# One transfer for four partition groups, and rings of rows without repeated rows, in an involution-like convolution layer

## The chip, the cores and the metric

The kernel runs on one core of a Trainium2 chip. The metric is the device time of one execution in microseconds (us). Before the change the median of three timed runs is 3795.8 us (3777.51 to 3800.52). One more execution was recorded by the hardware profiler; its own time is 3790.98 us, and the page and the trace spoken of below are of that one.

## The reference

The program has two layers. The first is the one the change is in. For each image it normalises `x` by groups, makes three 1x1 convolutions `x1` (32 channels), `x2` (32) and `x3` (256), and computes a weight for each of 49 neighbours of each pixel. The weights are shared by the 8 channels of a group.

```
sub2 = x1[:, :, None] - unfold_patches(x2)          # 7x7 neighbours, reflected edges
feat = concat([sub2, subp])                         # subp: the same of two position planes
y    = relu(bn1(feat));  y = conv1x1(y, cw1)
y    = relu(bn2(y));     wgt = softmax(conv1x1(y, cw2) + cb2, over the 49 neighbours)
out += x3p[:, :, i:i+56, j:j+56] * wgt[:, :, idx]   # for the 49 (i, j), x3p = x3 padded
x    = x + out
```

There are 4 images of 256 channels and 56 x 56 pixels. The second layer is attention and a routed feed-forward network over the pixels as tokens. The change does not touch it.

## The kernel before

**The 49 neighbours.** The 128 partitions are four groups of 32 channels. Group g holds the same channels for another neighbour: a slot is a place (ki, kj) and a way, and group g of it works on kj+g (way `COLUMN`) or ki+g (way `ROW`). Twelve slots (`SLOTS`) of four groups are 48 neighbours. The 49th, the centre, is worked on apart: the functions named `..._own`.

**Blocks.** An image is cut into 14 blocks of 4 rows; 56 blocks in all. One round of a block reads the planes of `x1` and `x2`, takes differences (GpSimd), makes the hidden layer and the logits (TensorE into the PSUM tile `quad`, ScalarE out of it), the softmax, and then for each slot a product of a window of `x3` with the weights (`product_t`: eight slots on VectorE, the four of `POOLS` on GpSimd) which TensorE sums over the groups into `acc` (`add_t`). `divide` takes the sum out of `acc` into the tile `o`, `more` adds `x`, and `store` writes the block to `xs`.

**Planes in HBM, rings in SBUF.** For every 8 rows of an image `planes` computes `x1`, `x2` and `x3`, and `store_both` and `store_values` write them, padded, to `a12d` and `x3d` in HBM. The blocks load them back shifted by group: `rows_kept` fills the rings `xc` and `xw` (windows of `x3` for the two ways, 8 channels per partition) and `ac` (of `x2`). A ring keeps 12 rows, and its first three rows a second time behind them, so that every window of 4 rows is contiguous. Each load is four transfers, one for each group of 32 partitions, because each group reads from another offset. Every transfer is issued by SyncE's queue. `load_own` loads the middle row group of `x3` once more (`x3c`), for the centre's product, and the block's part of `x` (`xr`).

One transfer already has another form: `a1`, `aq` and the main transfer of `store_values` each move all 128 partitions, and the side of the transfer that lies in HBM is written as four groups of 32 rows. This is the main one of `store_values`:

```
bass.AP(to.tensor, to.offset, [[2 * PITCH, 4], list(to.ap[0]), [1, 2 * PITCH]])
```

**The order.** Every step of a round has a place in the table `AT`, in units of which a round has `ROUND` = 238. Step s of block k stands at `k * ROUND + AT[s]`; all steps are sorted by it and written down in that order, and each engine and SyncE's queue keep it (`InOrder`). Because the recording helper issues every operation, nearly all of them have its line, L946, in the profile; tiles tell them apart. On SyncE's queue the transfers of several blocks and of the next image's planes lie one behind another, stores among loads, and a transfer that waits holds up those behind it.

Of the kernel before, what the change touches and what calls it, by code (L numbers as in the profile page):

```python
# [58 lines left out]
def bn_affine(nc, pool, par, n, eps, tag):  # L59
# [25 lines left out]
KEPT = 12  # L85
RING = KEPT + 3
# [14 lines left out]
ROUND = 238  # L101
AT = {
    "load_places": -32, "load_relation": -13, "load_planes": -5, "differ_0": 0, "differ_1": 8,
    "differ_2": 11, "normal_0": 14, "normal_1": 19, "bend_0": 27, "differ_3": 31, "values_0": 43,
    "keep_values_0": 70, "differ_own": 81, "bend_1": 87, "load_statistics": 93, "stats": 98,
    "both": 104, "bend_own": 118, "hidden_0": 140, "keep_both": 151, "edges_both": 175,
    "bend_more_0": 179, "hidden_1": 201, "bend_more_1": 214, "load_second": 215, "logits_0": 227,
    "hidden_own": 241, "largest_0": 244, "bend_more_own": 253, "store_both": 253,
    "logits_own": 258, "logits_1": 264, "keep_own": 264, "values_1": 267, "largest_1": 271,
    "keep_values_1": 278, "most": 287, "lower_own": 290, "edges_values": 292, "spread_most": 316,  # L110
    "keep_most": 319, "lowered_0": 334, "exp_0": 343, "lowered_1": 344, "weights_0": 352,
    "load_first": 352, "store_values": 354, "weights_1": 355, "product_0": 360, "exp_own": 362,
    "product_1": 364, "product_2": 370, "exp_1": 373, "weights_3": 384, "add_up": 391,
    "product_5": 391, "weights_4": 393, "product_3": 394, "add_0": 410, "weights_6": 433,
    "invert": 435, "add_1": 436, "spread_inverse": 444, "add_3": 445, "product_4": 448,
    "keep_inverse": 458, "load_third": 466, "product_6": 479, "add_2": 484, "weights_7": 485,
    "add_6": 491, "product_8": 494, "add_5": 497, "weights_9": 500, "product_7": 504,
    "load_own": 505, "product_11": 514, "add_4": 519, "weights_10": 527, "product_own": 528,
    "product_9": 530, "product_10": 537, "add_8": 540, "add_7": 555, "shift_own": 565,
    "add_own": 574, "add_9": 580, "add_11": 587, "add_10": 592, "divide": 603, "more": 672,  # L120
    "store": 760,
# [4 lines left out]
def conv_layer(ctx: ExitStack, tc: tile.TileContext, d, xs: bass.AP, ln0: bass.AP):  # L126
# [72 lines left out]
    held = {}  # L199
# [80 lines left out]
    def planes(n, q):  # L280
# [92 lines left out]
        def store_values():  # L373
            stag = made.pop("x")
            to = x3d[n, :, (PAD + 8 * q) * PITCH : (PAD + 8 * q) * PITCH + 1]
            sy.dma_start(
                bass.AP(to.tensor, to.offset, [[2 * PITCH, 4], list(to.ap[0]), [1, 2 * PITCH]]),
                stag.rearrange("p h s w -> p (h s w)"),
            )
            for i in range(PAD):  # L380
                for copied, row, to in ((over, PAD - i, i), (under, 6 - i, WP - PAD + i)):
                    if copied:
                        sy.dma_start(
                            x3d[n, :, to * PITCH : (to + 1) * PITCH],
                            stag[group(row // 2), row % 2].rearrange("p s w -> p (s w)"),
                        )
# [35 lines left out]
    mean_w = const.tile([P, P], F32, name="mean_w")  # L422
# [8 lines left out]
    xc = rings.tile([P, RING, SH, WP], F32, name="xc")  # L431
    xw = rings.tile([P, RING, SH, WP], F32, name="xw")
    ac = rings.tile([P, RING, WP], F32, name="ac")
# [3 lines left out]
    quarters = lambda a, n, j: a[n].rearrange("(l j s) f -> j l s f", j=4, s=2)[j]  # L437
# [7 lines left out]
    def rows_kept(n, quads, ring, of, way):  # L445

        count = ROW_QUADS if way == ROW else COL_QUADS
        height = WP - PAD if way == ROW else WP
        pitch = of.shape[-1] // WP
        every = pitch if way == ROW else 1  # L450
        ring = ring.rearrange("p h s w -> p (h s w)" if ring is not ac else "p h w -> p (h w)")
        todo, quads = [], list(quads)
        while quads:
            at = (count * n + quads[0]) * 4 % KEPT
            m = min(len(quads), (KEPT - at) // 4)
            rows = min(4 * m, height - 4 * quads[0])
            todo.append((at, 4 * quads[0], rows))
            quads = quads[m:]
        for at, r, rows in list(todo):
            if at == 0:  # L460
                todo.append((KEPT, r, min(rows, RING - KEPT)))
        for at, r, rows in todo:
            for g in range(4):
                size = rows * pitch - (g if way == COLUMN else 0)
                from_ = r * pitch + g * every
                sy.dma_start(
                    ring[group(g), at * pitch : at * pitch + size], of[:, from_ : from_ + size]
                )

    def first_row(k, t):  # L470

        ki, _, way = SLOTS[t]
        n, b = blocks[k]
        return (4 * ((ROW_QUADS if way == ROW else COL_QUADS) * n + b) + ki) % KEPT

    def load_relation(k):
        n, b = blocks[k]
        at = (b * RB + PAD) * WP
        a1 = ap.tile([P, RB, WP], F32, tag="a1", name=f"a1_{k}")
        src = a12d[n, :, 0, at : at + RB * WP]  # L480
        sy.dma_start(
            a1.rearrange("p h w -> p (h w)"),
            bass.AP(src.tensor, src.offset, [[0, 4], list(src.ap[0]), [1, RB * WP]]),
        )
        rows_kept(n, [b + 2] if b else range(3), ac, a12d[n, :, 1], COLUMN)
        aw = ap.tile([P, WINDOW, WP], F32, tag="aw", name=f"aw_{k}")
        for g in range(4):
            off = (b * RB + g) * WP
            sy.dma_start(
                aw[group(g)].rearrange("p h w -> p (h w)"),  # L490
                a12d[n, :, 1, off : off + WINDOW * WP],
            )
        aq = ap.tile([P, 2, W], F32, tag="aq", name=f"aq_{k}")
        for i in range(2):
            src = a12d[n, :, i, at + PAD : at + PAD + 1]
            sy.dma_start(
                aq[:, i],
                bass.AP(src.tensor, src.offset, [[WP, RB], list(src.ap[0]), [1, W]]),
            )
# [9 lines left out]
    def load_first(k):  # L509
        n, b = blocks[k]  # L510
        rows_kept(n, [b + 2 if b else 0], xc, x3d[n], COLUMN)

    def load_second(k):
        n, b = blocks[k]
        if b == 0:
            rows_kept(n, (1, 2), xc, x3d[n], COLUMN)
        if b == 0:
            rows_kept(n, [0], xw, x3d[n], ROW)

    def load_third(k):  # L520
        n, b = blocks[k]
        rows_kept(n, [b + 1], xw, x3d[n], ROW)

    def load_own(k):
        n, b = blocks[k]
        at = b * RB + PAD
        x3c = xrp.tile([P, RB, 2, WP], F32, tag="x3c", name=f"x3c_{k}")
        xr = xrp.tile([P, 2, FB4], F32, tag="xr", name=f"xr_{k}")
        for j in range(4):
            sy.dma_start(  # L530
                x3c[group(j)].rearrange("p h s w -> p h (s w)"),
                x3d[n].rearrange("l (h f) -> l h f", f=PITCH)[
                    :, at : at + RB, 2 * j * WP : 2 * (j + 1) * WP
                ],
            )
        for j in range(4):
            sy.dma_start(
                xr[group(j)], quarters(x, n, j)[:, :, b * FB4 : (b + 1) * FB4]
            )
        held["x", k] = x3c, xr  # L540

    def relation(k):
# [4 lines left out]
        def differ(i):  # L547
# [5 lines left out]
            else:  # L553
                r = first_row(k, t)
# [11 lines left out]
        def differ_own():  # L566
            aq = held["a", k][2]
            c = held["c1", k] = smp.tile([P, W], F32, tag="c1", name=f"c1_{k}")
            gp.tensor_tensor(c, aq[:, 0], aq[:, 1], ALU.subtract)
# [56 lines left out]
    def softmax(k):  # L626
# [42 lines left out]
        def lower_own():  # L669
            w = held["rw", k] = smp.tile([P, 2, W], F32, tag="rw", name=f"rw_{k}")  # L670
            ve.tensor_tensor(
                w[:, 1], held["mm", k][:, 2], held["mx", k], ALU.subtract
            )

        def exp_own():
            w = held["rw", k][:, 1]
# [27 lines left out]
        def add_up():  # L704
# [9 lines left out]
            for q in range(4):  # L714
                te.matmul(
                    small[group(q), :W], spreads[:, q, :REL], held["rw", k][:, 1], start=False,
# [3 lines left out]
        def invert():  # L720
            z = smp.tile([P, W], F32, tag="z", name=f"z_{k}")
            ve.tensor_reduce(z, view(small, 0, [[1, W], [W, 4]]), AX.X, ALU.add)
            ve.reciprocal(held["rw", k][:, 0], z)

        def spread_inverse():
            rw = held["rw", k]
            for q in range(4):
                for j in range(4):
                    te.matmul(
                        view(small[group(j)], q * W, [[FB4, 2], [1, W]]),  # L730
                        spreads[:, q, group(j)], rw, start=True, stop=True,
                        skip_group_check=True,
                    )

        def keep_inverse():
            r = held["rzs", k] = smp.tile([P, 2, FB4], F32, tag="rzs", name=f"rzs_{k}", bufs=1)
            se.activation(r.rearrange("p i f -> p (i f)"), small[:, : 2 * FB4], AF.Identity)
# [24 lines left out]
    def values(k):  # L762
# [7 lines left out]
        def product(t):  # L770
# [8 lines left out]
            (ve if ours else gp).tensor_tensor(  # L779
                pr.rearrange("p s (h w) -> p s h w", w=W),  # L780
                (xw if way == ROW else xc)[:, r : r + RB, :, kj : kj + W].rearrange(
                    "p h s w -> p s h w"
                ),
# [1126 lines left out]
```

## Time and profile before

| | |
|---|---|
| median of three timed runs | 3795.8 us |
| profiled execution: own time, span | 3790.98 us, 3789.2 us |
| convolution layer, from the start to the last `divide` | 1891 us |
| attention and feed-forward, after it | 1898 us |
| PE, DVE, ACT, POOL busy over the span | 84%, 63%, 42%, 46% |
| bytes moved by DMA, mean rate | 376.40 MB, 99 GB/s |

The span runs from the first to the last of the program's instructions. PE is TensorE, DVE VectorE, ACT ScalarE, POOL GpSimd, SP SyncE. The page's DMA share is the mean busy share of the core's 16 DMA engines, so four busy engines make 0.25. The busy shares are means over two layers with different limits, so they say little of the convolution alone; the windows over parts of the span do.

### The profile page before, as it was taken

The numbers are of one execution on the slowest core, as the hardware profiler recorded it, in microseconds if no ns is written. First come the engines' busy times: TensorE is split into PE (matmuls) and PEld (weight loads), VectorE is DVE, ScalarE is ACT, GpSimd is POOL, SyncE is SP. The second block draws the span as 40 slices with busy tenths as digits, with TensorE's granted clock in tenths as the row PEclk, the third lists the DMA queues.
The fourth block names the chain that finished last, engine by engine and source line by source line (L and its number), as shares of the span: only waits on it lengthen the run. The fifth ranks groups of instructions, "written<-read, shape, count | busy, mean of one in ns | idle before, by whom it ended". The sixth has DMA issues, their size and how long they took to land. (4 is left out here: it accounts for less than half of the span.)

```text
span 3789.2 us, 124795 instructions
## 1 busy us (share of the span) xinstructions
PE 3182.8 (84%) x55008; PEld 1437.2 (38%) x55008; DVE 2390.2 (63%) x3050; ACT 1585.4 (42%) x2880; POOL 1758.1 (46%) x1165
## 2 busy tenths in 40 slices
PE   2888876788678895898889988998899889979989
PEld 1333322333233342333244334333433344336666
DVE  2688666787678884788865557655665476534211
ACT  2455544454345453454324543454244424532111
POOL 0677656776577775788752015122421153111311
PEclk7899888899889897999989999999999999989999
DMA  5666656666666665666410220122012200231110
GB/s 142 154 165 148 165 127 156 165 151 155 146 161 159 160 144 135 158 163 157 111 66 20 63 53 27 29 77 61 29 22 73 68 24 12 60 94 44 53 50 27
DMA packets 251148, 376.40 MB, mean 99 GB/s; under 512 B 108041, under 2 KB 216237, under 8 KB 250221
## 3 DMA queue, kind: packets, MB, share of 16 engines
q1 hardware_dynamic: 236413, 333.79, 36.4%
q0 software_dynamic: 11408, 32.32, 2.7%
q8 instruction: 431, 7.06, 0.8%
q10 hardware_dynamic: 2784, 2.30, 0.2%
q14 instruction: 112, 0.92, 0.1%
HBM read 299.06 MB, written 68.74 MB: 97 GB/s over the span
## 5 line engine op out<-in xcount | busy, mean ns | idle before, releaser
L946 PE MATMUL acc<-pr,same 128*32 128x448 f32 x5376 | 644.5, 575 | 133.8 <-POOL pr L946 71.2
L946 ACT ACTIVATE ph<-pg,unit 128x896 f32<-128x896 f32 x448 | 427.1, 1004 | 473.8 <-PE pg L946 473.2
L946 POOL TENSOR_TENSOR pr<-xc,w 128x1792 f32<-128x1792 f32 x112 | 413.4, 3702 | 218.6 <-ACT w L946 141.3
L946 POOL TENSOR_TENSOR pr<-xw,w 128x1792 f32<-128x1792 f32 x112 | 422.5, 3773 | 148.8 <-PE acc L946 124.4
L946 DVE TENSOR_TENSOR pr<-xc,exp 128x1792 f32<-128x1792 f32 x224 | 443.3, 1999 | 51.0 <-ACT exp L946 44.9
L946 DVE TENSOR_TENSOR pr<-xw,exp 128x1792 f32<-128x1792 f32 x224 | 445.2, 2007 | 0.0
L946 POOL TENSOR_TENSOR phi<-ls 128x512 f32<-128x512 f32 (+1 forms) x200 | 245.6, 1228 | 350.0 <-PE accs L946 184.5
L946 DVE TENSOR_TENSOR phi<-pv,ls 128x1408 f32<-128x1408 f32 (+1 forms) x200 | 321.9, 1619 | 64.9 <-PE accs L946 47.7
L946 PE MATMUL quad<-y,cw 32*32 32x448 f32 (+1 forms) x10752 | 308.9, 476 | 13.3 <-ACT w L946 5.9
L946 DVE TENSOR_REDUCE mm<-quad 128x56 f32<-128x1792 f32 x112 | 174.1, 1554 | 217.3 <-PE quad L946 212.8
L946 PE MATMUL pg<-qT,pairs 32*128 32x448 f32 x1792 | 275.0, 591 | 6.2 <-ACT ph L946 3.8
L946 POOL DMA_DIRECT2D out<-tk x28 | 20.9, 747 | 541.7 <-ACT tk L946 531.1
L946 PEld LDWEIGHTS acc<-pr,same 128*32 128x32 f32 x5376 | 147.0, 114 | 322.3 <-issue 131.7
L946 POOL TENSOR_TENSOR y<-a,ac 128x672 f32<-128x672 f32 x112 | 168.1, 1524 | 204.8 <-DMA a<-a12d 102.0
L946 PE MATMUL pv<-wqkv,xn 128*32 128x256 f32 x3136 | 218.3, 394 | 49.6 <-DVE phi L946 31.2
L946 ACT ACTIVATE ls<-pv 128x256 f32<-128x256 f32 (+1 forms) x200 | 77.5, 387 | 390.7 <-PE pv L946 347.8
L946 PE MATMUL accs<-phi,v 128*32 128x512 f32 (+1 forms) x1600 | 218.9, 611 | 23.2 <-DVE phi L946 22.2
L946 ACT ACTIVATE exp<-w 128x224 f32<-128x224 f32 x448 | 158.3, 357 | 179.8 <-DVE pr L946 178.3
L946 POOL DMA_INDIRECT us<-rows,to x112 | 110.6, 987 | 263.1 <-DMA us<-rows,to 232.4
L946 ACT ACTIVATE y<-quad,bn2t,bn2s 128x1792 f32<-128x1792 f32 x112 | 164.7, 1470 | 139.1 <-PE quad L946 136.9
L946 PE MATMUL acc<-ph,cf 128*32 128x448 f32 (+1 forms) x1792 | 215.5, 553 | 0.0
L946 ACT ACTIVATE w<-quad,par 128x1792 f32<-128x1792 f32 x112 | 154.5, 1379 | 104.5 <-PE quad L946 101.5
(273 smaller groups left out, 5393.6 us busy)
## 6 DMA issues: line engine op xcount, KB each, us to landing
xw<-x3d SPq DMA_DIRECT2D x224, 248.0 KB
xw<-x3d SPq DMA_DIRECT2D x96, 186.0 KB
x3d<-sx SPq DMA_DIRECT2D x28, 496.0 KB
x3c<-x3d SPq DMA_DIRECT2D x224, 62.0 KB
xc<-x3d SPq DMA_DIRECT2D x54, 248.0 KB
xc<-x3d SPq DMA_DIRECT2D x54, 247.9 KB
xc<-x3d SPq DMA_DIRECT2D x54, 247.8 KB
xc<-x3d SPq DMA_DIRECT2D x54, 247.6 KB
```

The source lines that it names most:

```text
L946: return lambda *a, **k: self.tc.keep_in_program_order(of(*a, **k))
```

## The change

- `rows_kept` becomes `rows_shifted`: one transfer for all four groups, the HBM side written as four groups of 32 rows. The loads of `aw`, `ac`, `xc` and `xw` use it, and `store` writes a block in two transfers of 128 partitions in place of four of 32.
- `xc` keeps 20 rows and `xw` 16, without a second copy of the first three. A window that goes past the end of the ring is cut: `product` then issues two instructions, and a quad (4 rows) is loaded one block earlier.
- The centre's product reads row `PAD` of the ring `xw` in a layout of [group: row, 8 channels], so `x3c` is no longer loaded. Its sum takes 16 small matmuls in place of 4, and the inverse is spread once and not with a second weight beside it.
- `xr` is loaded from an input that the host lays out by block, in one contiguous transfer of 128 partitions. `aq` has one part in place of two.
- New places (`AT`, `ROUND` = 236); an image's planes are prepared six rounds ahead, not four; the statistics of image 1 run at twice the pace.

```diff
-KEPT = 12
-RING = KEPT + 3
+COL_KEPT, ROW_KEPT = 20, 16
+AC_KEPT = 12
+AC_RING = AC_KEPT + 3
...
-ROUND = 238
+ROUND = 236
...
-    def rows_kept(n, quads, ring, of, way):
...
-        for at, r, rows in list(todo):
-            if at == 0:
-                todo.append((KEPT, r, min(rows, RING - KEPT)))
-        for at, r, rows in todo:
-            for g in range(4):
-                size = rows * pitch - (g if way == COLUMN else 0)
-                from_ = r * pitch + g * every
-                sy.dma_start(
-                    ring[group(g), at * pitch : at * pitch + size], of[:, from_ : from_ + size]
-                )
+    def rows_shifted(n, r, rows, to, of, way):
...
+        size = rows * pitch - (PAD if way == COLUMN else 0)
+        sy.dma_start(
+            to[:, :size],
+            spread_out(
+                of, r * pitch, [[pitch if way == ROW else 1, 4], list(of.ap[0]), [1, size]]
+            ),
+        )
+
+    def load_quad(i, way):
+        count, height, kept, ring = (
+            (ROW_QUADS, WP - PAD, ROW_KEPT, xw) if way == ROW else (COL_QUADS, WP, COL_KEPT, xc)
+        )
+        n, q = divmod(i, count)
+        rows = min(4, height - 4 * q)
+        at = 4 * i % kept
+        rows_shifted(
+            n, 4 * q, rows, ring[:, at : at + rows].rearrange("p h s w -> p (h s w)"), x3d, way
+        )
...
     def load_relation(k):
...
-        for g in range(4):
-            off = (b * RB + g) * WP
-            sy.dma_start(
-                aw[group(g)].rearrange("p h w -> p (h w)"),
-                a12d[n, :, 1, off : off + WINDOW * WP],
-            )
...
+        rows_shifted(n, b * RB, WINDOW, aw.rearrange("p h w -> p (h w)"), a12d, ROW)
...
     def load_own(k):
         n, b = blocks[k]
-        at = b * RB + PAD
-        x3c = xrp.tile([P, RB, 2, WP], F32, tag="x3c", name=f"x3c_{k}")
-        xr = xrp.tile([P, 2, FB4], F32, tag="xr", name=f"xr_{k}")
-        for j in range(4):
-            sy.dma_start(
-                x3c[group(j)].rearrange("p h s w -> p h (s w)"),
...
-        held["x", k] = x3c, xr
+        xr = held["x", k] = xrp.tile([P, 2, FB4], F32, tag="xr", name=f"xr_{k}")
+        sy.dma_start(xr.rearrange("p s f -> p (s f)"), d["x_own"][n, b])
...
         def spread_inverse():
-            rw = held["rw", k]
-            for q in range(4):
-                for j in range(4):
-                    te.matmul(
-                        view(small[group(j)], q * W, [[FB4, 2], [1, W]]),
-                        spreads[:, q, group(j)], rw, start=True, stop=True,
-                        skip_group_check=True,
-                    )
+            spread(held["rz", k])
...
+            ring, kept = (xw, ROW_KEPT) if way == ROW else (xc, COL_KEPT)
+            rest = max(0, r + RB - kept)
+            for h, at, rows in ((0, r, RB - rest), (RB - rest, 0, rest)):
+                if rows:
+                    f = slice(h * W, (h + rows) * W)
+                    (ve if ours else gp).tensor_tensor(
...
         def product_own():
-            pr = made["own"] = smp.tile([P, 2, FB4], F32, tag="po", name=f"po_{k}", bufs=1)
+            pr = made["own"] = smp.tile([P, SH, W], F32, tag="po", name=f"po_{k}", bufs=1)
+            r = (4 * (ROW_QUADS * n + b) + PAD) % ROW_KEPT
             ve.tensor_tensor(
-                pr.rearrange("p s (h w) -> p s h w", w=W),
-                held["x", k][0][:, :, :, PAD : PAD + W].rearrange("p h s w -> p s h w"),
...
+                pr, xw[:, r, :, PAD : PAD + W],
+                held["wo", k].unsqueeze(1).to_broadcast([P, SH, W]), ALU.mult,
             )
...
         def store():
-            xr = held.pop(("x", k))[1]
-            f = slice(b * FB4, (b + 1) * FB4)
-            for j in range(4):
-                sy.dma_start(quarters(xs, n, j)[:, :, f], xr[group(j)])
+            xr = held.pop(("x", k))
+            for s in range(2):
+                sy.dma_start(channels(xs, n, b, s), xr[:, s])
...
-            at = (per * n + 2 * q - 4) * ROUND
+            at = (per * n + 2 * q - 6) * ROUND
```

## The prediction

> **What bounds the kernel now.** First the windows, the convolution and what follows it, then a good and a bad stretch inside the convolution (columns: stretch, its length, busy time and instructions of each engine, granted clock, DMA share, GB/s).
>
> ```profile
> 95.00:1891.00 1796.00, 1445.31 (x33772) 605.31 (x33756) 1370.99 (x996) 851.97 (x1521) 1260.74 (x561) 0.91 0.64 151
> 1891.00:3789.20 1898.20, 1713.58 (x20718) 815.76 (x20718) 999.27 (x1996) 714.29 (x1319) 491.05 (x595) 0.96 0.17 48
> 1600.00:1800.00 200.00, 179.68 (x4223) 73.96 (x4217) 176.52 (x118) 102.82 (x185) 163.18 (x74) 0.95 0.68 158
> 400.00:600.00 200.00, 143.43 (x3256) 59.47 (x3255) 129.48 (x104) 87.36 (x154) 117.46 (x54) 0.85 0.59 142
> ```
>
> The convolution has 56 blocks in 1796 us, 32.1 us each. A block holds 1445 / 56 = 25.8 us of PE, 1371 / 56 = 24.5 us of DVE and 22.5 us of POOL. In the good stretch all three are 82 to 90% busy: the engines bound it together. In the bad one (the end of image 0) they wait. No DMA limit shows: the share is 0.64. But that is a mean over sixteen engines, and the change alters how many of them a transfer uses. So the second view is SyncE's queue around one transfer of the form that the change gives to the rest, then windows inside it, and one while `xc` is loaded by group.
>
> ```profile
> 653.14 0.54 SPq L946 DMA_DIRECT2D x3d<-sx  x1
> 662.69 0.38 SPq L946 DMA_DIRECT2D ln<-lt  x1
> ```
>
> ```profile
> 654.00:659.00 5.00, 4.80 (x103) 1.44 (x91) 5.00 (x4) 4.74 (x6) 1.71 (x2) 1.00 0.26 55
> 659.00:662.60 3.60, 3.22 (x96) 1.46 (x112) 3.60 (x4) 2.33 (x6) 2.05 (x1) 1.00 0.19 74
> 1321.00:1324.00 3.00, 3.00 (x72) 2.45 (x68) 2.90 (x5) 0.00 (x0) 2.77 (x2) 0.60 0.99 243
> ```
>
> Between 653.7 and 662.7 nothing else is issued. The main transfer of `store_values` (128 partitions, HBM side as four groups of 32 rows, 496 KB) keeps a share of 0.26: four engines of sixteen. A group's load (32 partitions, one group) keeps 0.99 busy at 243 GB/s. The trace's semaphore records say the same of the other transfers of this form: each of the 56 loads of `a1` and of the 28 of these stores updates its semaphore five times (four engines, as I read it, and once for the rest), a load of `xc`, `xw` or `aw` sixteen times. The DMA view names them:
>
> ```profile
> xw<-x3d SPq DMA_DIRECT2D x224, 248.0 KB
> x3d<-sx SPq DMA_DIRECT2D x28, 496.0 KB
> a<-a12d SPq DMA_DIRECT2D x56, 124.0 KB
> ```
>
> **The merged transfers.** After the change `xc`, `xw`, `ac`, `aw` and the store to `xs` have this form. From the code, in the whole convolution: `xc` 60 transfers of 128 runs of 7,924 B and 4 of half that, 62.9 MB; `xw` 56 of 128 x 7,936 B and 4 of three quarters, 59.9; `aw` 12.4; `ac` 9.8; `a1` 7.1; `aq` 1.6; `xs` 12.8; the stores to `x3d` 14.2. That is 180.7 MB on four engines. The stores to `a12d` (4.6 MB) update three times, so by the same reading they use two engines and weigh twice on theirs: 9.2. The rest (`xb`, `xa`, `xr`, first image: 45.6 MB) is spread over sixteen, a quarter of it on the four: 11.4. Sum: 201.2 MB for the four busiest engines. By the same count the kernel before has 24.5 + 9.2 + 249.0 / 4 = 96 MB there.
>
> The price per byte. Below: the window at 659 us has 74 GB/s at 0.19, so 24.3 GB/s for each busy engine and 97 for four. Above: the window at 654 us has 55 GB/s at 0.26, 13.2 per engine, and four at 55 GB/s. In between, where I go: the 2,816 packets of 3,968 B of these stores between 400 and 1800 us took 190 ns in the mean by the trace's packet records, 20.9 GB/s an engine, 84 for four. I take it because it is the mean of this very form beside the kernel's other traffic.
>
> 201.2 MB at 84 GB/s is 2395 us, or 42.8 us a block. The first store to `x3d` is issued at 48.7 us; after the last load a block's products are still to be made, about 25 us by DVE's 24.5 us a block. Convolution end: 49 + 2395 + 25 = 2469 us, against 1891. Adding the unchanged 1898 us and the 1.8 us between span and own time: 2469 + 1898 + 2 = **4370 us**, 579 more than the profiled 3790.98 (itself 5 below the median).
>
> [...]
>
> **What lies beside this at no cost**, as long as four engines need 42.8 us a block and no compute engine more than 26:
>
> - Repeated rows: 80 and 96 transfers of 186 KB go, and `x3c` with 224 of 62 KB, some 48 MB that were spread over sixteen engines. The wait for `x3c`, below, goes; what is late next is `xw`, which `product_own` now reads.
> - SyncE's queue issues 752 transfers in the convolution in place of 2240, at 0.4 to 0.55 us: about 700 us of issue. It had time for this. Now it waits for landings instead (third line).
> - `product_own` has the same 448 elements; 1.94 us before, 0.61 at best (that is `o<-acc`, of equal size): a gain of 0 to 1.3 us. The spread of the inverse falls from 16 x 262 to 16 x 221 ns, -0.7 us; `add_own` goes from 4 x 553 to about 16 x 262 ns, +2.0 us on PE; `keep_inverse` -0.1 us on ACT.
> - 51 products on DVE and 37 on POOL are cut in two; a cut costs between nothing and the 0.34 us of DVE's smallest reduction of 168 elements, at most 88 x 0.34 / 56 = 0.5 us a block.
> - New places and planes two rounds earlier: the stalls at the image ends (second and fourth window) cost 1796 - 33772 x 200 / 4223 = 196 us. They lie beside the DMA time now, and in the rival below they are the gain.
>
> If the cover is gone, these together are +1.8 us on PE and -0.8 to +0.5 on DVE a block, some 100 us in all.
>
> ```profile
> POOL y L946 <- DMA a<-a12d: 102.0, 6, 30.5
> DVE po L946 <- DMA x3c<-x3d: 87.7, 7, 27.6
> SPq L946 <- DMA xc<-x3d: 123.8, 159, 2.9
> ```
>
> A wait is added where `product_11` on POOL needs the quad of `xw` that `load_third` issues 13 units ahead of it; on the queue that load stands behind the store of two blocks before, the `xc` quad and the planes' stores. Behind `product_11` stand the next blocks' `differ` on POOL, for which ACT's `bend` and PE's `hidden` wait. In time it is not a second cost: two rounds of transfers (86 us) are longer than 0.65 of a round of transfers up to `xw` and the 25 us of products after it, so the four engines don't run dry.
>
> **Rivals.**
>
> - All sixteen engines carry the merged transfers, and the kernel is faster. Then 231 MB at 243 GB/s are 950 us and hidden, the image ends go smoothly, and the convolution runs at the pace of 1600 to 1800 us: 3791 - 196 = 3595 us, 3650 with half of the compute costs above. For it: runs of 7.9 KB are long, and the gain in issue is real. Against: 0.26, and the five updates of `a1`, which has the same form in the same direction. It decides as soon as a merged load shows a share near 1; the limit for no loss is 201.2 / (1891 - 74) = 111 GB/s on the busiest four, which no row reaches. Chance 0.10.
> - Four engines in step. [...] If loads of all four groups stay in step the price is the upper one: 201.2 MB at 55 GB/s, 3658 us, and 5630 us in total. Between 84 and 55 there is much room; from 68 GB/s down, 0.12. [...]
> - Four engines at their best, 97 GB/s: 2074 us and 4050 us in total. It is the lower part of my case; faster than 99 GB/s, 0.04. No change within 1% would need 108 GB/s or engines that are bound to the same time by chance: 0.02.
>
> **How the numbers follow.** The likeliest case, 68 to 99 GB/s, has 0.72: 4370 us, and 4000 to 4950 at its ends. The range is these ends, with 0.10 below as the first rival and 0.12 above. Three runs before spread by 0.6%, so 1% is about what a measurement tells from no change. Faster 0.10, same 0.02, slower 0.88.
>
> **What would show it.** In the profile after: a DMA share of about 0.25 to 0.35 over the convolution in place of 0.64, with 90 to 100 GB/s; a share of 0.25 while `xw` or `xc` is loaded; products that wait for `xc` and `xw` at the head of the waits; DVE still about 24 us busy a block of over 40; the part after the convolution within 1% of 1898 us. The prediction is wrong if a merged load's share is near 1, if the four engines carry well over 97 or under 68 GB/s, or if the queue stops for something else, such as a ring's rows not yet read, so that the four engines idle.

## The result and the profile after

The changed kernel takes 4110.3 us (median; 4093.8 to 4131.0), the kernel before, timed beside it, 3796.4 us (3777.5 to 3800.5). The ratio is 1.085, 95% interval 1.080 to 1.090: the kernel became slower by 314 us. The profiled execution took 4130.95 us at a span of 4129.0, against 3789.2 before.

First the windows of the changed kernel: the convolution from its first `divide` to its last, the rest, and a short stretch in which little but one merged load of `xw` runs; then the convolution of the kernel before, also from its first `divide` to its last (columns as before: stretch, length, busy time and instructions of each engine, granted clock, DMA share, GB/s).

```profile
218.00:2231.00 2013.00, 1456.73 (x34014) 601.85 (x34010) 1287.72 (x1024) 812.58 (x1474) 1221.41 (x583) 0.84 0.31 108
2231.00:4129.00 1898.00, 1710.30 (x20721) 814.46 (x20718) 999.84 (x1996) 714.37 (x1319) 491.40 (x595) 0.97 0.17 48
654.00:659.00 5.00, 5.00 (x162) 2.40 (x155) 4.34 (x3) 2.11 (x5) 1.16 (x2) 1.00 0.26 108
```

```profile
154.00:1891.00 1737.00, 1402.29 (x32836) 586.06 (x32820) 1340.13 (x973) 826.87 (x1479) 1228.68 (x546) 0.91 0.64 151
```

All of the loss is in the convolution: its last `divide` starts at 2231 us in place of 1891, and the 1898 us after it are the same to the microsecond. The first `divide` is 64 us later (217.8 against 153.6), and from there to the last one a block takes 36.6 us in place of 31.6. The compute engines have little more to do or less (PE 1457 us against 1402, DVE 1288 against 1340, POOL 1221 against 1229) in a convolution that is 276 us longer. The DMA share is halved, from 0.64 to 0.31, while the kernel waits for DMA: as much as five of sixteen engines, four of them and a share of the transfers that are spread over all. In the third row it is 0.26 at 108 GB/s.

Of the waits, those for loads of the rings, of the planes and of `x2` (columns: who waited for what, us in total, times, longest).

```profile
ACT xb L962 <- DMA xb<-in_x: 451.6, 25, 91.2
POOL pr L962 <- DMA xw<-x3d: 409.7, 54, 16.2
...
POOL y L962 <- DMA ac<-a12d: 160.1, 29, 10.8
...
DVE pr L962 <- DMA xw<-x3d: 107.2, 25, 12.3
```

GpSimd's products wait for a quad of `xw` 54 times in 56 blocks. The wait for `x3c`, 87.7 us before, is gone with its load. The transfers that answer to the three shown of before are these (x count, KB of each):

```profile
xc<-x3d SPq DMA_DIRECT2D x60, 990.5 KB
xw<-x3d SPq DMA_DIRECT2D x56, 992.0 KB
x3d<-sx SPq DMA_DIRECT2D x28, 496.0 KB
```

By the trace's semaphore records the loads of `xc`, `xw`, `ac` and `aw` now have five updates each, as `a1` had before. By its packet records, from the second block's `divide` to the last but one, 3.73 of four packets of the merged sizes are in flight in the mean, and none in 1.5% of the time: the four engines are never long without work. SyncE's queue, around one block (columns: start in us, duration):

```profile
1100.47 0.57 SPq L962 DMA_DIRECT2D xw<-x3d  x1
1101.09 0.54 SPq L962 DMA_DIRECT2D a<-a12d  x1
1101.74 2.90 SPq L962 DMA_DIRECT2D ac<-a12d  x1
1104.69 9.22 SPq L962 DMA_DIRECT2D aw<-a12d  x1
```

An issue that took 0.4 to 0.55 us before can now take 9.22 us, here at a share of 0.27 and 104 GB/s (1104.7 to 1113.9 us), so with the four engines at work. SyncE has fewer transfers to issue, but such an issue holds it up.

### The profile page after: what moved, and what is told of

The parts are those of the page before. It is cut to its first block, busy times and chain, and to the rows that moved or that the text cites. A ratio compares the mean times of both kernels' runs of the same rounds, so it can differ in the third digit from the quotient of the medians.

```text
span 4129.0 us, 125672 instructions
## 1 busy us (share of the span) xinstructions
PE 3235.2 (78%) x56352; PEld 1455.5 (35%) x56352; DVE 2339.8 (57%) x3101; ACT 1571.5 (38%) x2878; POOL 1750.9 (42%) x1202
## 5 line engine op out<-in xcount | busy, mean ns | idle before, releaser
L962 PE MATMUL acc<-pr,same 128*32 128x448 f32 x5376 | 664.0, 590 | 116.0 <-DVE pr L962 111.1
L962 DVE TENSOR_TENSOR pr<-xw,exp 128x1792 f32<-128x1792 f32 (+1 forms) x252 | 451.7, 1805 | 325.3 <-ACT exp L962 217.3
L962 POOL TENSOR_TENSOR pr<-xw,w 128x1792 f32<-128x1792 f32 (+2 forms) x126 | 417.3, 3313 | 502.0 <-DMA xw<-x3d 409.7
L962 DVE TENSOR_TENSOR pr<-xc,exp 128x1792 f32<-128x1792 f32 (+2 forms) x247 | 447.2, 1836 | 66.7 <-ACT exp L962 66.7
L962 PE MATMUL small<-xb,w 128*32 128x112 f32 (+1 forms) x3744 | 142.5, 301 | 411.8 <-ACT xb L962 399.5
L962 POOL TENSOR_TENSOR pr<-xc,w 128x1792 f32<-128x1792 f32 (+1 forms) x135 | 419.4, 3114 | 86.3 <-ACT w L962 56.8
L962 POOL TENSOR_TENSOR phi<-ls 128x512 f32<-128x512 f32 (+1 forms) x200 | 246.6, 1233 | 346.4 <-PE accs L962 181.6
L962 PE MATMUL quad<-y,cw 32*32 32x448 f32 (+1 forms) x10752 | 320.8, 503 | 91.9 <-ACT w L962 69.5
L962 PEld LDWEIGHTS small<-xb,w 128*32 128x32 f32 x3744 | 97.0, 116 | 476.3 <-ACT xb L962 437.6
L962 POOL DMA_DIRECT2D out<-tk x28 | 20.9, 748 | 544.3 <-ACT tk L962 533.6
L962 PEld LDWEIGHTS quad<-y,cw 32*32 32x32 f32 x10752 | 86.6, 109 | 365.9 <-issue 208.7
```

Source lines behind the costliest of these rows:

```text
L962: return lambda *a, **k: self.tc.keep_in_program_order(of(*a, **k))
```

## The experiments

The theory is that of the forecast: a merged transfer runs on as many engines as its HBM side has groups, four, and the bytes on these four set the time. The counts below (MB on the four busiest engines) are made as in the prediction. "Conv" is the start of the last `divide`. Each ratio is to the kernel before, timed on the same chip; the kernel before took 3785 to 3807 us on these chips, so times from different chips compare only to within some 20 us.

**1. All by group.** The kernel after, with the transfers of the old form; rings, places and the centre stay.

```diff
-        sy.dma_start(
-            to[:, :size],
-            spread_out(
-                of, r * pitch, [[pitch if way == ROW else 1, 4], list(of.ap[0]), [1, size]]
-            ),
-        )
+        per = 1 if pitch == PITCH else 1
+        for g in range(0, 4, per):
+            every = pitch if way == ROW else 1
+            sy.dma_start(
+                to[g * REL : (g + per) * REL, :size],
+                spread_out(of, r * pitch + g * every, [[every, per], list(of.ap[0]), [1, size]])
+                if per > 1
+                else spread_out(of, r * pitch + g * every, [list(of.ap[0]), [1, size]]),
+            )
...
-            for s in range(2):
-                sy.dma_start(channels(xs, n, b, s), xr[:, s])
+            for j in range(4):
+                sy.dma_start(
+                    spread_out(
+                        xs[n], b * FB4 + 2 * j * HW, [[SH * HW, REL], [HW, 2], [1, FB4]]
+                    ),
+                    xr[group(j)],
+                )
```

> The changed kernel with one part undone: the loads of xc, xw, ac, aw and the store to xs are four transfers again, one for each group of 32 partitions. Rings, places, centre's product and contiguous xr stay. Theory (four busiest engines set the round): the four carry 22.9 + 9.2 + (45.6 + 157.8) / 4 = 83 MB, under 900 us at the 93 GB/s that the changed kernel reaches, so the compute engines set the round again: convolution end 1700 to 1800 us, total 3600 to 3700 us, DMA share above 0.5. Rival (the new places and late loads of xw cost the time, not the number of engines): total stays above 4000 us, with products waiting for xw.

3686.9 us, ratio 0.974 (0.971 to 0.977), within the expected range. Its window over the convolution, and the row of `o` (duration, first and last start):

```profile
180.00:1798.00 1618.00, 1390.20 (x34012) 590.27 (x34002) 1289.04 (x1025) 810.57 (x1474) 1223.65 (x583) 0.94 0.55 134
```

```profile
L970 DVE TENSOR_TENSOR o<-acc,rzs x56: 608/612/627, 180.2 to 1798.0; 128x448 f32<-128x448 f32 x56
```

As many instructions as in the kernel after, the same busy time on DVE, ACT and POOL (PE 1390 us against 1457), and the same bytes, at a share of 0.55 in place of 0.31: 423 us less. The merging costs more than the whole loss; the rest of the change is a gain.

**2. Only the rings by group** (`xc`, `xw`; 109 MB on the four):

> The changed kernel with only xc and xw loaded by group again; ac, aw and the store to xs stay merged. Theory: 57.9 + 9.2 + (122.8 + 45.6) / 4 = 109 MB on the four busiest engines, 1170 us at 93 GB/s, still hidden, so within 2% of the kernel with everything by group. Rival (each merged transfer costs by its number or its latency, small ones too): clearly above that kernel, by 100 us or more.

3717.8 us, ratio 0.981 (0.978 to 0.984), conv 1829.1: within 0.9% of the first. The two rings carry nearly all of the loss.

**3. Only `ac`, `aw` and the stores to `xs` by group** (175 MB on the four, the large ones merged):

> The changed kernel with only ac, aw and the store to xs by group again; xc and xw stay merged. Theory: 201.2 - 0.75 x 35 = 175 MB on the four, at 93 GB/s 1880 us, convolution end about 1950 us, total 3800 to 3900 us: the time goes with the bytes on the four engines. Rival (the long latency of a merged ring load sets the round, whatever else the engines carry): total stays within 2% of 4110 us.

Both missed: 4284.1 us, ratio 1.131 (1.127 to 1.136), conv 2397.4. With 26 MB fewer on the four engines the kernel is slower than the kernel after. The window over the convolution and SyncE's own waits:

```profile
215.00:2397.00 2182.00, 1529.47 (x34011) 616.39 (x33980) 1313.02 (x1024) 810.86 (x1474) 1220.66 (x583) 0.81 0.33 99
```

```profile
SPq L970 <- DMA xw<-x3d: 272.0, 51, 10.3
SPq L970 <- DMA x3d<-sx: 120.2, 28, 5.3
```

In the kernel after the first of these is 9.1 us. Here SyncE stands still 51 times because an `xw` has not landed, and the four engines run dry: of the packets that still run on four engines 2.98 are in flight in the mean, and none in 18% of the time. Bytes are not all; runs 6, 9 and 12 ask what else counts.

**4. The rings in two transfers of two groups each** (HBM side of two groups, 64 partitions):

```diff
+        per = 2 if pitch == PITCH else 4
+        for g in range(0, 4, per):
...
+                to[g * REL : (g + per) * REL, :size],
+                spread_out(of, r * pitch + g * every, [[every, per], list(of.ap[0]), [1, size]])
```

> The changed kernel with xc and xw each loaded in two transfers of two groups (64 partitions, HBM side as two groups of 32 rows). Theory (the slowest dimension of the HBM side sets the number of engines): two engines each, and always the same two, so these carry 2 x 122.8 + 57.9 + 9.2 + 11.4 = 324 MB in the measure of four: 3480 us at 93 GB/s, total near 5450 us, and the semaphores of these loads are updated three times each. Rival (the number of engines follows from the size of a transfer, or two transfers take different engines): total at or below 4110 us, with a higher DMA share.

5200.9 us in one run, against 3785.1 of the kernel before; 249 us under the expected number, with packets of 7,924 bytes at 312 ns in the mean (344 in the kernel after).

```profile
273.00:3301.00 3028.00, 1648.43 (x34011) 641.11 (x33980) 1255.55 (x1024) 810.33 (x1474) 1219.49 (x583) 0.72 0.20 72
```

Half the groups on the HBM side, and the rings run on two engines: their semaphores are updated three times for each load, as expected, and two of their packets are in flight in 67% of the time, more than two in 2%. The share is 0.20 (two of sixteen are 0.125, and the transfers on four and sixteen come on top). So four groups went with four engines (five updates, 3.73 packets in flight in the kernel after) and two groups with two. The two halves share the same two, or they would have made four engines' work together.

**5. Three of every four ring rows.** The loads of `xc` and `xw` move three rows of a quad; a quarter of the ring stays zero, so the sums leave out what those rows bring. As many transfers, 172 MB.

```diff
+        if pitch == PITCH:
+            rows = min(rows, 3)
         size = rows * pitch - (PAD if way == COLUMN else 0)
```

> The changed kernel, each load of xc and xw moving three rows of its four (the fourth row of each quad stays zero, so a quarter of the ring rows is left out of the result); all transfers, places and waits stay in number and order. Theory (bytes on the four busiest engines set the time): 201.2 - 29.5 = 171.8 MB, at 93.3 GB/s 1841 us, convolution end near 1915 us, total 3815 us (3770 to 3870). Rival (each merged transfer's wait in the queue sets it, as one may suspect from the by-group small transfers that did not help): total within 2% of 4110 us.

3878.2 us, ratio 1.018 (1.016 to 1.020), conv 1979.4: 1.7% above the point and just over the range, far from 4110. 29.4 MB less bring 232 us. Of the merged sizes (the loads of `xc` now have packets of 5,940 bytes) 3.56 packets are in flight in the mean and none in 4.7% of the time, against 3.73 and 1.5% in the kernel after: the four engines still have work nearly all the time, and bytes explain most of the step.

**6. Eight small transfers a block more** (32 x 16 bytes each, into a tile that nothing reads), behind the load of `aq`:

```diff
         held["a", k] = aw, a1, aq
+        for i in range(8):
+            sy.dma_start(idle[group(i % 4), i // 4, k % 4], x[0, :REL, 4 * i : 4 * i + 4])
```

> The changed kernel with eight more transfers a block, of 32 partitions x 16 bytes into an unused tile, at the end of load_relation: no bytes to speak of, but as many more transfers on SyncE's queue as ac, aw and xs by group add. Theory (SyncE waits before it issues until a transfer some eight places earlier has landed; more transfers a block make it wait for the merged xw and xc, and the four engines run dry): total 4200 to 4300 us, with SyncE's waits for xw above 150 us against 9 in the changed kernel. Rival (by-group small transfers disturb the merged ones on the way into SBUF): total within 1% of 4110 us.

4425.4 us, ratio 1.162 (1.159 to 1.164), conv 2521.1. The direction held, the size did not, and the named wait was wrong: SyncE waits for `aw`, and not for `xw`.

```profile
SPq L965 <- DMA aw<-a12d: 106.7, 56, 2.1
SPq L965 <- DMA ac<-a12d: 26.7, 45, 1.1
```

Transfers of no weight cost 315 us, 0.7 us for each of 448. The waits shown are 133 us of that; the 448 issues themselves take SyncE 259 us.

**7. All sixteen.** The first, and also `a1`, the main stores to `x3d` and the stores to `a12d` by group (60 MB on the four, 1968 transfers in the convolution):

```diff
-        sy.dma_start(
-            a1.rearrange("p h w -> p (h w)"),
-            spread_out(a12d[n, :, 0], at, [[0, 4], l, [1, RB * WP]]),
-        )
+        for g in range(4):
+            sy.dma_start(
+                a1[group(g)].rearrange("p h w -> p (h w)"),
+                spread_out(a12d[n, :, 0], at, [l, [1, RB * WP]]),
+            )
...
```

> The kernel with everything by group, and also a1, the main store to x3d and the stores to a12d, which had used four or two engines before the change too, each by group of 32 partitions. Theory: a transfer of 508 KB that took 9 us of four engines takes some 3, and fewer landings hold up the queue: 3640 to 3680 us, at or below everything by group (3687). Rival (the number of transfers counts more by now, 1968 in place of 1660): 3700 us or more.

3683.1 us, ratio 0.967 (0.965 to 0.969), 3 us over the expected range. On another chip than run 1; runs 10 and 11 put the two side by side.

**8. The merge alone.** The kernel before, with `rows_kept`, `aw` and the stores to `xs` merged; rings with repeated rows, `x3c` and the old places stay (238 MB on the four, 1233 transfers).

> The kernel before with the merging alone: rows_kept, aw and the store to xs in one transfer for four groups (two for the store); repeated rows, x3c, places and everything else as before. Theory: with the repeated rows 237.9 MB lie on the four busiest engines, 2550 us at 93.3 GB/s, total near 4525 us, slower than the whole change. Rival (the loss is in the new rings or places): near the kernel before, within 3% of 3796 us.

4874.0 us in one run, against 3806.8 of the kernel before. The merge alone is the loss, 1067 us of it in the kernel before; the shorter rings without repeated rows soften it. It is also 349 us more than bytes alone gave, and SyncE waits for `xw` as in the third run:

```profile
SPq L952 <- DMA xw<-x3d: 261.2, 59, 10.5
```

**9. The eight small transfers behind the load of `xw`** in place of `aq`. By then I believed that SyncE could hand over a few merged transfers ahead and ran out of time behind `aq`.

> The kernel after, and the same eight small transfers a block as in the run with small transfers (4425 us), now issued right behind the load of xw, which has 992 KB on the four engines, in place of behind the small load of aq. Theory, the queue's room: SyncE can hand over only a few merged transfers ahead; behind aq the eight small issues (about 0.6 us each) come when little is left on the four engines, behind xw they come while some 10 us of work is left, and SyncE would wait there anyway (12 us after xw's issue at 1122 us of the kernel after). Then 4060 to 4200 us. Rival, a price per transfer on the engines or the queue wherever it stands, 0.65 us each: 4425 us again, 4360 to 4490.

4432.7 us, ratio 1.167 (1.163 to 1.171): the rival's number, as if a transfer had a price wherever it stands. But the queue shows why (SyncE's timeline), and what the DMA engines did in the meantime (windows):

```profile
1116.49 0.57 SPq L965 DMA_DIRECT2D xw<-x3d  x1
1117.11 16.35 SPq L965 DMA_DIRECT2D idle<-in_x  x8
1133.51 0.56 SPq L965 DMA_DIRECT2D a<-a12d  x1
```

```profile
1126.00:1130.00 4.00, 3.92 (x127) 1.86 (x119) 3.37 (x4) 1.58 (x5) 0.00 (x0) 1.00 0.28 109
1133.00:1135.00 2.00, 2.00 (x65) 1.51 (x67) 1.77 (x1) 1.76 (x1) 1.71 (x1) 1.00 0.05 4
```

The eight issues fill 16 us. Taken one by one from the trace, seven of them are issued by 1123.8 us; the eighth at 1133.15, 0.02 us after `xw` has landed (1133.13). Then nothing is left on the four engines: share 0.05 and 4 GB/s until the next loads begin. The trace names the semaphore of each transfer: SyncE's use eight in turn, so the eighth small one has the semaphore of `xw`, and the issuing instruction itself waits for that semaphore before it uses it. So the eight are a rule of this program; no run here shows a limit of the chip behind them. The same rule is seen in run 6 (around 1132 us the seventh small one follows the landing of `aw`, eight places before it, by 0.02 us) and in run 3 (at 1109.29 us a load of `ac` follows that of `xw`, eight places before it, by 0.02 us). In all traces no transfer of SyncE's queue is issued with more than seven before it still under way (seven at the end of 525 of 2912 issues in the kernel before, of 31 of 1422 in the kernel after). The view of waits says it in sum (for run 9; 9.1 us in the kernel after):

```profile
SPq L965 <- DMA xw<-x3d: 557.0, 57, 13.7
```

**10, 11. The first and the seventh beside each other.**

> The kernel after with xc, xw, ac, aw and the stores to xs by group, for a comparison on one chip with the next run. Theory: 3665 to 3700 us, ratio to the kernel before 0.971 to 0.977.

> The same with a1, the main stores to x3d and the stores to a12d by group as well. If the four engines still cost something with 83 MB on them (1598 us between the start of the stores and the last o of the first such run, against 690 us at 120 GB/s), this is below the run beside it by over 0.5%; if not, within 0.5% of it, since its 308 further issues cost nothing either on a queue that waits.

3703.7 us (3695.7 to 3705.3), ratio 0.974 (0.971 to 0.977), against 3690.3 us (3678.1 to 3705.9), ratio 0.971 (0.967 to 0.975): 0.4% apart, with runs that overlap; the first is 4 us over its expected range. With 83 MB on them the four engines cost nothing that these runs can tell. (No row shows the 120 GB/s of the expectation for four engines; at 93.3 the 83 MB take 890 us, still far less than 1598.) Both beat the kernel before and the kernel after.

**12. The small transfers of run 9 issued by GpSimd.** GpSimd's transfers have eight semaphores of their own (111 to 118 in the traces of the kernels before and after, where SyncE's have 99 and 101 to 107).

```diff
-            sy.dma_start(idle[group(i % 4), i // 4, k % 4], x[0, :REL, 4 * i : 4 * i + 4])
+            gp.dma_start(idle[group(i % 4), i // 4, k % 4], x[0, :REL, 4 * i : 4 * i + 4])
```

> The eight small transfers stand where they stood in the run with them behind xw (4433 us), but GpSimd's queue issues them and not SyncE's. Theory: SyncE's transfers take eight semaphores in turn and each waits until the one eight places before it has landed; in the run behind xw the eighth small one was issued at 1133.15 us, 0.02 us after xw had landed, with the four engines empty. GpSimd's queue has eight semaphores of its own, so nothing of this is left: 4090 to 4200 us, the upper part for GpSimd, whose DMA issues take 0.75 to 1 us each in the kernel after, 6 to 8 us more a block on an engine that had about 22 of 36.6 us. Rival, a price per transfer on the DMA engines, whoever issues it (0.7 us each): 4430 us, 4380 to 4490.

4120.4 us, ratio 1.086 (1.082 to 1.090), as the kernel after and in the expected range. The same bytes at the same place cost nothing; the whole block of eight takes GpSimd 4 us, and the four engines are full again (3.73 of four, none in 1.6% of the time).

```profile
1129.48 3.97 POOL L965 DMA_DIRECT2D idle<-in_x  x8
```

```profile
218.00:2231.00 2013.00, 1451.34 (x34028) 602.91 (x34020) 1286.71 (x1031) 811.87 (x1474) 1439.15 (x1032) 0.84 0.32 111
```

GpSimd's queue sends these bytes as other packets (of 32 bytes and 4, where SyncE's has 16 and 4), so run 12 alone does not show that SyncE's packets cost the DMA engines nothing. The packet records of run 9 do: those of 16 bytes take 8 ns each, some 7 us of each engine in the whole convolution. So the 0.7 us for each small transfer is no price of the DMA engines. It lies in SyncE's queue. In run 9 it is the room: eight transfers, whatever their size, and waits for `xw` of 557 us where the loss is 322. In run 6 the waits for room come to 133 of the 315 us. What is left may be SyncE's own 259 us for the small issues; no run separates the two, since run 12 takes both off SyncE, and at the place of run 9.

## Why the prediction was right, and where it was off

**Four engines: held.** The forecast shares of 0.25 to 0.35 in the convolution and 0.25 while a ring is loaded were 0.31 and 0.26; the 90 to 100 GB/s became 108, with what the other engines carry. Run 1 took the groups off the HBM side of the same bytes and the loss became a gain; run 4 halved the groups, and with them the size of a transfer: a load's updates went from five to three and the time up by 1090 us. The rival with sixteen engines is out for the merged kernel. Its time, 3595 to 3650, was meant for the change without the DMA limit, and runs 1 and 7 come to 3687 and 3683. Their convolution ends 93 us (run 1) before that of the kernel before, about half of the 196 us put down to the image ends; ACT still waits 204.6 us for `xb` there (230.8 before), so the image ends are only in part smooth.

**The price of a byte: the mis-sized term.** 201.2 MB at 84 GB/s were to take 2395 us and end the convolution at 2469. From the same sum (2231 - 49 - 25) they took 2157 us, 93.3 GB/s (92.9 from the trace's own ends, the first store at 50.2 us and the last landing of a ring's load at 2215.9). The difference, 238 us, is the whole miss of 4370 against the profiled 4131; against the median, 4110, it is 260. The packets say the same: those of `xc`, 7,924 bytes, took 344 ns in the mean between 400 and 1700 us, 23.0 GB/s an engine and 92 for four. The 20.9 GB/s I took were a mean over packets of 3,968 bytes; these had a median of 160 ns and a mean of 190 in the kernel before, and a median and a mean of 162 in the kernel after. The mean before was pulled up by a tail of slow packets.

The loads by group beside the stores are not the cause of that tail. The two stores that run alone, at 653.1 and 720.0 us, have 228 ns in the mean; those at 422.7, 783.0 and 968.0 us, with loads by group beside them, 168 or 169. A store has the tail in full when nothing else is on the engines as it begins. In run 9, where no load is by group, 13 of the 20 stores between 100 and 1800 us begin so, with 234 to 236 ns in the mean. In the kernel after one of 23 does, at 190.4 us, with 235 ns; the others have 161 to 165. That one has 47 GB/s in its first 5 us and 91 behind them (windows of the kernel after):

```profile
191.00:196.00 5.00, 5.00 (x134) 2.22 (x124) 4.91 (x6) 3.67 (x6) 5.00 (x3) 1.00 0.24 47
196.00:200.00 4.00, 4.00 (x100) 1.47 (x92) 4.00 (x3) 1.54 (x4) 4.00 (x2) 1.00 0.25 91
```

So the forecast priced engines that are always at work by a row with slow starts in it; the reason given for the row, that it stands beside the kernel's other traffic, was the wrong one. Why such a start is slow was not tried. The median would have given 99 GB/s, 6% too much in place of 10% too little.

**In step at 55 GB/s: out as a lasting price, seen as a slow start.** The very window between 654 and 659 us has 108 GB/s at a share of 0.26, and no fortieth of the span within the convolution has less than 91 on the page. The slow rate is there, as above, for the first 5 us of a store that begins alone; that engines in step are its reason is not shown, and the packet records speak against it. In the kernel before the first four packets of the store at 653.1 us begin within 0.13 us of one another (654.32 to 654.45) and take 192 to 302 ns; but at 659.59 us, too, four begin within 0.07 us, and take 154 ns each. Over the whole convolution 93.3 GB/s were measured.

**"The four engines don't run dry": held, and with luck.** Of SyncE's queue I counted the issues that go (1488) as time it had anyway. The issues that are left are longer, though: 695 of them take 1382 us between the first and the last `divide`, where 2114 took 1051 before. And the reason I gave for the engines, two rounds of transfers ahead, leaves out that no transfer is issued here with more than seven before it still under way. The kernel after needs about 13 transfers a block and is at 3.73 of four. With 21 to 23 a block (runs 3, 6, 8, 9) SyncE waits for landings in the middle of a block, and in runs 6, 8 and 9 some 0.7 us are lost for each added transfer. It made no difference to this forecast, and it made my expectations of runs 3, 6 and 8 too low: by 380 to 480, 125 to 225 and 349 us.

**No cost where I said none.** DVE's work between the first and the last `divide` is 1288 us (1340 before), 23 us a block; cut products and the 16 matmuls of `add_own` do not show, in run 1 either, where the cover is gone (PE 1390 us, 1402 before). The part after the convolution is 1898.0 us against 1898.2. Near the head of the waits is `xw`, as said, while `xc` has 30.0 us; that for `xb` stands above it. The planes' loads queue behind the merged ones, which may be why; no run tried it.

**What stays open.** The 9.22 us of `aw`'s issue in the kernel after are not the eight semaphores: the transfer eight places before had landed 10 us earlier, and three to seven were under way at the end of such long issues. Something else holds SyncE up inside an issue while the four engines are full; what it is was not tried.

## What to carry to other kernels

Fewer and larger transfers were no gain here: look at how many groups the HBM side of a transfer is written as. Transfers of 1 MB whose HBM side was four groups of 32 rows had 93 GB/s on four engines, with two groups a load ran on two (run 4), and four transfers of 248 KB with 32 rows each, by group, were 423 us better in this kernel (run 1), though SyncE issued some 900 more. When a kernel's DMA share is low and its engines wait for DMA, multiply the share by 16 to see how many engines are at work (0.31 were five here), before you call the transfers hidden. And count places on the queue as well as bytes: in this program, whose queue has eight semaphores, no more than seven others were issued behind a large transfer (in run 9 the eighth small one went 0.02 us after `xw` had landed), and small ones cost nothing on GpSimd's queue (run 12, 4120.4 us against 4110.3).

## What the runs showed of the hardware that I had not expected

- Four engines on long runs carry 92 to 103 GB/s (344 ns in the mean, 307 in the median, for 7,924 bytes on one engine), 10 to 23% more than the mean of the shorter packets of before had suggested.
- A store on four engines that begins with the engines idle has about half its later rate for some 5 us (47, then 91 GB/s in the kernel after at 191 us; 55, then 74 before at 654, with a share of 0.19 in the second: 13.2, then 24.3 for each busy engine). Behind other transfers it has no such start (162 ns a packet against 235).
- A packet of 7,924 bytes takes longer where the loads run on sixteen engines: 595 ns in the mean in the kernel before (400 to 1700 us) and 544 in run 1, 344 in the kernel after. The engines are slower one by one (13.3 GB/s in the kernel before against 23.0) and faster together: 243 GB/s at a share of 0.99 at 1321 us of the kernel before, 108 at 0.26 at 654 us of the kernel after.
- The issue of a transfer can itself take 9.22 us while the engines behind it are full; the window over the long one (1104.7 to 1113.9 us, share 0.27, 104 GB/s) shows nothing else amiss.
